# Two orders of work rewritten in an eight-layer kernel: the stores and loads beside the filters of the first mixer, and the pieces carried beside the scans of the last

## The chip, the cores and the metric

The kernel runs on one core of a Trainium2 chip, as one program. The metric is device microseconds of one execution on that core, lower being better. The time of a kernel is the median of several runs; for the kernel before there are three.

## What is computed

Eight layers follow one another on `x` of shape (8, 512, 256): eight sequences of 512 tokens with 256 features. Each layer `f` adds to the residual, and layernorm stands on both sides of it:

```python
x = x + _layernorm(f(_layernorm(x, axis=-1), *weights), axis=-1)
```

There are four pairs of a mixer and a feed-forward layer. Two mixers, and the feed-forward layer between the third mixer and the fourth, matter here. The first mixer has three causal filters of 3, 15 and 63 taps for each of its 256 features, a delta rule in chunks whose triangular matrix is inverted, and a softmax gate over five paths that mixes the results:

```python
local_s, local_m, local_l = _fir(v_direct, fir_s), _fir(v_direct, fir_m), _fir(v_direct, fir_l)
...
        T = solve_triangular(M, jnp.broadcast_to(eye, M.shape), lower=True)
...
o = probs[..., 0:1] * local_s + probs[..., 1:2] * local_m + probs[..., 2:3] * local_l \
    + probs[..., 3:4] * delta_out + probs[..., 4:5] * v_direct
```

The last mixer is a selective state space model with 512 channels (DI) and 16 states. For each sequence:

```python
xr = x @ W_in.T
xc, res = (xr[..., :DI], xr[..., DI:])
u = silu(causal_conv4(xc) + b_conv)
x_dbl = u @ W_xproj.T                       # dt (16), B (16), C (16)
delta = softplus(dt @ W_dt.T + b_dt)
dA = exp(delta * A);  dBu = delta * B * u   # for each state n
h = dA_t * h + dBu_t                        # over the tokens t, for each channel and state
y = sum over n of h * C  +  u * D
out = (y * silu(res)) @ W_out.T
```

(The last block is shortened from the reference.) The feed-forward layer ahead of it, called the guest below, is `h = silu(x @ wg.T) * (x @ wu.T)`, `out = h @ wd.T`, with integer weights that are scaled by 1/127. All arithmetic is float32.

## The kernel before

The kernel keeps `x` in SBUF and writes out the program layer by layer. PE, DVE, ACT, POOL and SP each run their own list of instructions in order, and wait on semaphores for one another. Transfers are issued from SP's list, and some from ACT's. A scheduler puts the traced instructions into those lists. Two means of the code fix parts of the order. `behind()` (L375) asks that what is traced under it comes, on SP, DVE, ACT and POOL, after the instruction of that engine that was traced last. `in_order()` (called at the end of `l3_attn`) makes the order in which the last mixer is traced the order of the lists of PE, DVE, ACT and POOL.

**The filter stage** is in `l0_attn`. Its loop runs over G = 32 groups `g`. `filters(g)` does 16 matmuls of 128x256 elements (L661) into two PSUM tiles, multiplies each by its gates on DVE (`pr`, L666), loads the band matrix of group g + 3 (`load_band`: SP issues 256 KB at L452 and 320 KB at L455), adds the parts on POOL (`s1` L672, `s2` L674) and stores `s2` by two DMAs that ACT issues (L676). The first two bands have buffers of their own; the others share three, by g modulo 3. Beside the filters the loop carries, under `behind()`, other parts of the mixer:

- `scaled_v` (ACT L645, store L648): one tile `vs` a step.
- `strengths(1)` (iterator `late`), `gates`, `query_scales`, `value_scales`: small work on row vectors.
- `inverse(g)` (L328), a generator that `next()` advances piece by piece. It inverts the triangular matrices of one half of the sequences. Its pieces are: loads (SP L331, 2 MB, and a small one); one and then another DVE instruction; 15 pieces that hold two pairs of DVE instructions each; a last DVE product that yields True; the upper triangle cleared on POOL (affine_select L361) and the diagonal copied (L364); a 2 MB store from SP (L366) together with the first of four transposed copies on ACT (`tt`, L369) and its 512 KB store from ACT; and the other three copies and stores, one a piece.
- The first half's inverse is done up to True before the stage. In the stage, `inv` is advanced in steps g = 1 (affine_select), 5 (2 MB store and first transposed store) and 6, 7, 8 (the other three); the call of step 9 ends it. In step 7 the second half's `inverse(1)` starts with its loads, and from step 11 on it advances by one piece a step, on DVE.
- In step 10 the loads for the next stage are issued: `load_tt` for sequences 0 and 1 (POOL memsets L413 and L414, two SP loads L417 each) and `load_blocks` (SP L426, L429, L432).

**The last mixer** is `l3_attn`. It runs the eight sequences one after another, each in 32 steps p: two halves h of the channels, times 16 states n. A step k of the whole chain does, in this order: `fetch(k + 4)` (SP loads the rows C and B, spread over the partitions); `scan(k, 0)`, for the first 128 channels, that is a decay dA on ACT (L2069, into PSUM pool `pA` with two buffers) and the scan on DVE (L2081); `spread(k + 2)`, the product dB; about half of the list `now`; `scan(k, 1)`; `weigh(k)`, the product with C on POOL (L2085, 2.4 us); the rest of `now`; the `pieces(b, p)` of the step; and `summed(k - 2)`, transposes on PE that add up y in PSUM (L2098). In `spread`, dB of n even, 7 or 15 is done on DVE (1.2 us), after ACT has copied B into PSUM (`pb`, L2062); for the other n it is done on POOL (2.4 us).

`pieces(b, p)` is a timetable. It names for each step the parts of other work that run beside the scans of sequence b: parts of b itself (`own`), of the next sequence a = b + 1 (`nxt`), of the one before, z = b - 1 (`last`: its gating, transposes and output projection), of the guest's sequence f = b + 2 (`ffn`), and of g = b + 3 (`later`). A part issues its matmuls at once and returns a list of functions for what follows them; these are the list `now` of the next step, and may return further lists for the step after. The order of the lists inside a step is the order in which `pieces` adds them: `last`, the burst of p = 22, `out`, `nxt`, `ffn`, `later`, `own`.

The parts that the change names or that work beside them are:

- `delta(b, c)`: one matmul (pd, L1967), then on ACT Abs, Relu and Exp (L1973, one step later), Identity and Ln (a step later), then three DVE instructions `third` (a step later). pd keeps its PSUM buffer until the third of these.
- `drive(b, h)`: du = delta * u on POOL.
- `turn_g(b, h)`: the transposes of the gated y on PE into two PSUM tiles pg, copied by ACT a step later.
- `project(b, m)`: eight matmuls (po, L2028), copied by ACT (L2031) a step later.
- `rest(b, h, m)`: the matmuls for `res`, copied a step later. `hidden(b, c, j)`: the guest's gate and up products (pf, L1883), copied by ACT (hid, L1889) a step later. `out_stats`, `norm_*` and `moments`: layernorm statistics on DVE, ACT and POOL (lnb, L1848); `scaled` (L1853): x times the scale on ACT.

All of these PSUM tiles (pd, pg, po, pf and the others tagged "mm") come from the pool `pmm` with three buffers. In step 22 `burst` does the decays of steps 23 and 24 ahead of time into SBUF tiles T[0] and T[1], and then all SiLUs of the next sequence and of the guest in one group on ACT. In step 23 the list `now` is held back by a step, and in step 24 its first function is put last.

Of the kernel before, what the change touches and what calls it, by code (L numbers as in the profile page):

```python
# [9 lines left out]
F32 = mybir.dt.float32  # L10
# [9 lines left out]
P = 128  # L20
NB = 8
# [253 lines left out]
def l0_attn(K):  # L275
    nc, tc = K.nc, K.tc
    w = K.W["l0_attn"]
    W = w[:, 0:2 * A_END].rearrange("p (k n) -> p k n", k=2)
    row = w[:, 2304:2332]
    H, J, G = 4, 8, 32  # L280
    HALF = NB // 2
    with ExitStack() as es:
# [152 lines left out]
        with ExitStack() as e1:  # L435
# [23 lines left out]
            with ExitStack() as ef:  # L459
                p1, p2, p3 = pool(ef, "a", 1), pool(ef, "b", 2), pool(ef, "d", 3)  # L460
# [102 lines left out]
                inv = iter(())  # L563
# [16 lines left out]
            with ExitStack() as ef:  # L580
# [13 lines left out]
                for g in range(2, 5):  # L594
                    load_band(g)

                gz = rw_all[:, 0:20, :].rearrange("p (h f) t -> p h f t", h=H)
# [44 lines left out]
                def scaled_v(b, n):  # L642
                    vs = p2.tile([P, H, 64], F32, tag="vs", name=f"vs{b}_{n}")
                    for h in range(H):
                        nc.scalar.mul(  # L645
                            vs[:, h, :], Vw[:, b, 2 * n + 1, 64 * h:64 * h + 64],
                            SSK[:, b, n, h:h + 1])
                    nc.scalar.dma_start(  # L648
                        out=v_d[b * P:(b + 1) * P, 256 * n:256 * n + 256],
                        in_=vs.rearrange("p h d -> p (h d)"))  # L650

                def filters(g):
# [19 lines left out]
                    nc.gpsimd.tensor_tensor(s1, pr[:, :, 0:2, :], pr[:, :, 2:4, :], ALU.add)  # L672
                    s2 = p2.tile([P, 4, 64], F32, tag="s2", name=f"s2_{g}")
                    nc.gpsimd.tensor_tensor(s2, s1[:, :, 0, :], s1[:, :, 1, :], ALU.add)  # L674
# [7 lines left out]
                for g in range(G):  # L682
                    filters(g)
                    with behind():
# [7 lines left out]
                        if g in (0, 4, 6):  # L692
                            next(late, None)
                        if g in (1, 5, 6, 7, 8, 9):
                            next(inv, None)
                        if g == 7:
                            inv2, inverted = inverse(1), False
                            next(inv2)
                        if g == 10:
                            assert next(inv, 0) == 0  # L700
                            for b in range(2):
                                load_tt(b)
                            load_blocks(0, TS0, T10)
# [1072 lines left out]
def l3_attn(K):  # L1776
# [10 lines left out]
    with ExitStack() as es:  # L1787
# [234 lines left out]
        def project(b, m):  # L2022
            R[b]["Y"] = flat(T[1])
            ps = pmm.tile([P, 2, D], F32, tag="mm", name=f"po{b}_{m}")
            for j in range(2):
                n = 2 * m + j
                for c in range(4):
                    nc.tensor.matmul(  # L2028
                        ps[:, j, :], lhsT=R[b]["g", c // 2][:, c % 2, n * P:(n + 1) * P],
                        rhs=W[:, c, M_OUT:M_OUT + D], start=(c == 0), stop=(c == 3))  # L2030
            return [lambda: nc.scalar.copy(R[b]["Y"][:, 2 * m:2 * m + 2, :], ps)]  # L2031

# [21 lines left out]
        def spread(k):  # L2054
            if k < len(order):
# [3 lines left out]
                on = nc.gpsimd  # L2059
                if n % 2 == 0 or n in (7, 15):  # L2060
                    pb = pB.tile([P, L], F32, tag="b", name=f"pb{b}_{h}_{n}")
                    nc.scalar.copy(pb, B)  # L2062
                    B, on = pb, nc.vector
# [63 lines left out]
        def pieces(b, p):  # L2127

            a, z, f, g = b + 1, b - 1, b + 2, b + 3
            own = {0: [(delta, b, 2)], 3: [(delta, b, 3), (open_sums, b, 0)],  # L2130
                   6: [(drive, b, 1), (rest, b, 1, 0)], 9: [(rest, b, 1, 1)],
                   19: [(open_sums, b, 1)], 20: [(turn_g, b, 0)]}
# [5 lines left out]
                   20: [(rest, a, 0, 0)], 21: [(rest, a, 0, 1)],  # L2138
                   23: [(rows_of, a)], 24: [(delta, a, 0)], 25: [(delta, a, 1)],
                   28: [(drive, a, 0)]}  # L2140
            ffn = {1: [(hidden, f, 0, 0)], 2: [(hidden, f, 1, 0)], 3: [(hidden, f, 2, 0)],
# [8 lines left out]
            if b == 0:  # L2150
                for p0, p1 in ((1, 6), (2, 7), (3, 8), (4, 9), (5, 10)):
                    ffn[p1] = ffn.pop(p0)
                ffn.update({0: [(norm_stats, f)], 1: [(norm_root, f)], 2: [(norm_apply, f)],
                            4: [(turn_x, f, "fT")]})
            last = {5: [(turn_g, z, 1)], 7: [(project, z, 0)], 8: [(project, z, 1)],
                    10: [(out_stats, z)], 12: [(out_add, z)]}
# [9 lines left out]
            if f < NB:  # L2166
                todo += ffn.get(p, [])
            if g < NB:
                todo += later.get(p, [])
# [500 lines left out]
```

## Time and profile before

| what | us |
|---|---|
| runs shown, median (lowest to highest of 3) | 4557.25 (4557.15 to 4561.31) |
| the profiled execution, its time | 4555.24 |
| the same execution, its span | 4553.5 |

The span reaches from the first instruction to the last of one profiled execution; the mean granted clock of TensorE in it is 0.93. Over the span PE is busy 3963.8 us (87%), DVE 2698.8 (59%), ACT 2016.2 (44%) and POOL 2118.9 (47%). By stretches of the span, in us of busy time:

| stretch | long | PE | DVE | ACT | POOL | DMA share |
|---|---|---|---|---|---|---|
| 0 to 239, front of the first mixer | 239.0 | 199.6 | 174.9 | 128.8 | 5.7 | 0.39 |
| 239 to 402, the filter stage | 163.0 | 122.2 | 122.7 | 44.1 | 83.2 | 0.72 |
| 402 to 690, the delta rule and after | 288.0 | 245.4 | 154.2 | 109.9 | 76.5 | 0.54 |
| 690 to 2657, layers between | 1967.0 | 1772.7 | 1030.3 | 803.2 | 830.6 | 0.18 |
| 2657 to 2793, opening of the last mixer | 136.4 | 103.2 | 28.7 | 54.4 | 16.3 | 0.12 |
| 2793 to 3891, its eight sequences | 1097.6 | 898.5 | 967.8 | 731.5 | 941.4 | 0.38 |
| 3891 to the end, last layer | 662.5 | 622.2 | 220.3 | 144.3 | 165.3 | 0.50 |

"DMA share" is the mean busy share of the core's 16 DMA engines. The eight sequences of the last mixer take 146.9, 137.4, 136.4, 136.2, 136.6, 136.2, 150.0 and 117.9 us.

How to read the views: an instruction is named by its engine and line (DVE L2081), its output and inputs, and its tile's shape. A timeline lists runs of like instructions with their start, their length, how many (x), and in square brackets the engine's idle time just before and what ended it. A list of waits adds up, for one kind of instruction, the idle time that one releaser ended: the total, how many times, and the longest. SPq is SP's own list, and an entry of it is the issue of a DMA. Matmuls are pipelined, so a busy PE is not always PE at its peak.

### The profile page before, as it was taken

What the parts mean: (1) busy time and instruction counts of PE and PEld (TensorE: products, weight loads), DVE (VectorE), ACT (ScalarE), POOL (GpSimd) and SP (SyncE); (2) the same over time, 40 slices, a digit from 0 to 9 for tenths busy, and PEclk for the clock granted to TensorE, in tenths of its full rate; (3) what the DMA queues carried; (4) which work ended last, traced back from release to release, by engine and by line L of the source; (5) the groups of instructions that cost most, each with busy time, mean ns of one, the idle gap of its engine ahead of it and who ended that gap; (6) DMA issues with size and microseconds to landing.
All of it is one profiled execution on the core that took longest, in us unless ns stands there. A gap on an engine that the chain in (4) does not pass through costs nothing. (4 is left out here: it accounts for less than half of the span.)

```text
span 4553.5 us, 63426 instructions
## 1 busy us (share of the span) xinstructions
PE 3963.8 (87%) x21672; PEld 2633.7 (58%) x21672; DVE 2698.8 (59%) x7145; ACT 2016.2 (44%) x4210; POOL 2118.9 (47%) x2081
## 2 busy tenths in 40 slices
PE   8868888999998599699999978998888876899997
PEld 3435765555655499544554534565655545678884
DVE  7767656456757611255566534888888899721115
ACT  5532433444344233334444444767676655311112
POOL 0045222444344244344555423889988879223321
PEclk9889999999999799889999989899999886899999
DMA  4377621000000299400000002343433334336653
GB/s 120 94 218 189 179 62 63 5 5 7 7 10 16 69 254 251 130 5 10 6 6 6 1 23 68 123 125 126 127 122 122 124 110 136 103 118 234 228 180 113
DMA packets 392818, 442.90 MB, mean 97 GB/s; under 512 B 147853, under 2 KB 275967, under 8 KB 391983
## 3 DMA queue, kind: packets, MB, share of 16 engines
q1 hardware_dynamic: 361087, 390.18, 28.4%
q0 software_dynamic: 16272, 31.87, 2.6%
q10 hardware_dynamic: 15136, 16.80, 1.1%
q8 instruction: 172, 2.82, 0.3%
q14 instruction: 151, 1.24, 0.1%
HBM read 372.49 MB, written 66.26 MB: 96 GB/s over the span
## 5 line engine op out<-in xcount | busy, mean ns | idle before, releaser
L2085 POOL TENSOR_TENSOR h<-h,C 128x1024 f32<-128x1024 f32 x256 | 613.3, 2408 | 135.3 <-DVE h L2081 87.8
L2081 DVE TENSOR_TENSOR_SCAN h<-dA,dB 128x512 f32<-128x512 f32 x480 | 568.4, 1209 | 90.2 <-ACT dA L2069 73.9
L1039 POOL TENSOR_SCALAR p<-p,rs 128x128 f32<-128x128 f32 (+3 forms) x256 | 275.8, 1085 | 417.3 <-DVE rs L1038 261.1
L2069 ACT ACTIVATE dA<-dl,A 128x512 f32<-128x512 f32 x480 | 330.3, 690 | 174.4 <-DVE h L2081 173.7
L1605 DVE CUSTOM_DVE_ANT_0 junk<-S,mask 128x256 f32<-128x256 f32 (+3 forms) x512 | 249.5, 487 | 195.0 <-PE S L1599 156.7
L2098 PE MATMUL y<-C,h 128*128 128x128 f32 x2048 | 298.4, 297 | 68.0 <-POOL h L2085 67.9
L2098 PEld LDWEIGHTS y<-C,h 128*128 128x128 f32 x2048 | 263.2, 155 | 155.3 <-POOL h L2085 98.6
L1633 ACT ACTIVATE PT<-T 128x128 f32<-128x128 f32 (+3 forms) x512 | 198.0, 435 | 278.5 <-PE T L1628 267.6
L1599 PE MATMUL S<-KZ,QT 64*128 64x512 f32 (+3 forms) x1024 | 260.9, 492 | 23.9 <-DVE mx L1605 23.6
L2297 PE MATMUL gb<-xbT,w_b 128*128 128x256 f32 (+1 forms) x1472 | 255.3, 332 | 1.0 <-ACT ts L2501 0.6
L2297 PEld LDWEIGHTS gb<-xbT,w_b 128*128 128x128 f32 x1472 | 230.4, 191 | 22.8 <-ACT ts L2501 0.8
L2303 DVE TENSOR_TENSOR hTb<-sb,gb 128x512 f32<-128x512 f32 x71 | 48.8, 687 | 325.4 <-PE gb L2297 325.4
L2064 POOL TENSOR_TENSOR dB<-du,B 128x1024 f32<-128x1024 f32 x96 | 234.0, 2437 | 0.1
L1883 PE MATMUL pf<-fT,w_l_ffn 128*128 128x512 f32 x384 | 208.3, 681 | 26.5 <-ACT fT L1877 10.4
L1628 PE MATMUL T<-QT,KZ 64*128 64x384 f32 (+3 forms) x1024 | 216.7, 464 | 2.9 <-ACT PT L1633 2.5
L2064 DVE TENSOR_TENSOR dB<-du,pb 128x1024 f32<-128x1024 f32 x160 | 191.2, 1195 | 23.0 <-ACT pb L2062 21.2
L182 POOL TENSOR_TENSOR X<-X,yn 128x256 f32<-128x256 f32 (+1 forms) x56 | 79.4, 1436 | 255.3 <-ACT yn L177 213.9
L1373 ACT ACTIVATE hT<-h,w_l_ffn 128x128 f32<-128x128 f32 x384 | 109.5, 368 | 197.9 <-PE h L1368 197.9
L1368 PE MATMUL h<-xgT,w 128*128 128x128 f32 x1536 | 185.0, 279 | 0.0
L1636 POOL TENSOR_SCALAR_AFFINE_SELECT PT<-PT 128x512 f32<-128x512 f32 x128 | 81.2, 634 | 219.8 <-ACT PT L1633 206.8
L1599 PEld LDWEIGHTS S<-KZ,QT 64*128 64x128 f32 x1024 | 117.2, 193 | 113.9 <-issue 58.4
L2534 POOL DMA_INDIRECT ys<-yb,place x71 | 69.8, 984 | 238.7 <-ACT yb L2533 224.5
(605 smaller groups left out, 9266.5 us busy)
## 6 DMA issues: line engine op xcount, KB each, us to landing
w_b<-l3f_w SPq DMA_DIRECT2D x138, 512.0 KB
C<-xdd SPq DMA_DIRECT2D x256, 256.0 KB
B<-xdd SPq DMA_DIRECT2D x256, 256.0 KB
w<-l1f_w SPq DMA_DIRECT2D x48, 1024.0 KB
w<-l1f_w SPq DMA_DIRECT2D x48, 256.0 KB
band<-l0fd SPq DMA_DIRECT2D x30, 320.0 KB
X<-x SPq DMA_DIRECT2D x16, 512.0 KB
c<-ys SPq DMA_DIRECT2D x16, 512.0 KB
```

Source lines behind the costliest of these rows:

```text
L1039: nc.gpsimd.tensor_scalar(p[:, 0:n], p[:, 0:n], rs, None, ALU.mult)
L1599: nc.tensor.matmul(ps[:, 0:n], lhsT=QT[half, qt * P:n], rhs=KZ[half, j % 2, 0:n], start=True, stop=True)
L1605: nc.vector.tensor_tensor_reduce(out=junk[:, 0:n], in0=ps[:, 0:n], in1=mask[:, L - n:L], scale=1.0, scalar=-3.0e38, op0=ALU.add, op1=ALU.m ...
L1628: nc.tensor.matmul(ps[:, 0:n], lhsT=KZ[half, j % 2, kt * P:(kt + 1) * P], rhs=QT[half, kt * P:L], start=True, stop=True)
L1633: nc.scalar.activation(PT[:, j, :], ps[:, 0:n], AF.Exp)
L1883: nc.tensor.matmul(ps, lhsT=gu[:, k, j * 768 + c * P:j * 768 + (c + 1) * P], rhs=R[b]["fT"][:, k, :], start=(k == 0), stop=(k == 1))
L2064: on.tensor_tensor(dBs[k], R[b]["du", h], B[:, None, :].to_broadcast([P, 2, L]), ALU.mult)
L2069: nc.scalar.activation(dA, R[b]["dl", h][:, c, :], AF.Exp, scale=A[:, 2 * h + c, n:n + 1])
L2081: nc.vector.tensor_tensor_scan(hs[k][:, c, :], dA, dBs[k][:, c, :], 0.0, ALU.mult, ALU.add)
L2085: nc.gpsimd.tensor_tensor(hs[k], hs[k], row_C.pop(k)[:, None, :].to_broadcast([P, 2, L]), ALU.mult)
L2098: nc.tensor.matmul(R[b]["y", h][q // 2][:, q % 2, c * P:(c + 1) * P], lhsT=t[:, c, q * P:(q + 1) * P], rhs=K.ident, is_transpose=True, sta ...
L2297: nc.tensor.matmul(ps[:, q, :], lhsT=ww[:, k, (c + q) * P:(c + q + 1) * P], rhs=xT[:, k, :], start=(k == 0), stop=(k == 1))
```

## The change

It edits two functions and touches no arithmetic: the same products are made, two of them on another engine.

In the filter stage:

1. The piece of `inv` that holds the affine_select is advanced once before the loop, behind the loads of bands 2 to 4.
2. The other pieces of `inv` are advanced in steps 3, 5, 7 and 9 (2 MB store with the first transposed store, then the other three), and the call of step 11 ends it; before, in 5, 6, 7, 8 and 9.
3. `load_tt` and `load_blocks` are issued in step 13 instead of 10. The condition `g > 10` for the second inverse stays.
4. `vs` and `s2` have four buffers each instead of two.

In the last mixer:

5. `turn_g(z, 1)` moves from step 5 to 4, `project(z, 0)` and `project(z, 1)` from 7 and 8 to 6 and 7. The copy of the projection gets one more list around it, so it runs two steps after its matmuls instead of one, in steps 8 and 9 as before. `rest(b, 1, 0)` moves from 6 to 8.
6. `delta(a, 0)`, `delta(a, 1)` and `drive(a, 0)` of the next sequence move from steps 24, 25 and 28 to 25, 26 and 29, into a list `row` that is added behind the guest's list instead of ahead of it.
7. In half h = 1 the products of n = 10 and n = 11 change places: n = 10 (step 26, spread in step 24) goes to POOL without a copy pb, n = 11 (step 27, spread in step 25) to DVE with one.

```diff
--- before.py
+++ after.py
@@ -593,6 +593,8 @@
                     clear(bands[2 + i])
                 for g in range(2, 5):
                     load_band(g)
+                with behind():
+                    next(inv)
 
                 gz = rw_all[:, 0:20, :].rearrange("p (h f) t -> p h f t", h=H)
 
@@ -640,7 +642,7 @@
                     nc.vector.tensor_tensor(sk, sk, rk, ALU.mult)
 
                 def scaled_v(b, n):
-                    vs = p2.tile([P, H, 64], F32, tag="vs", name=f"vs{b}_{n}")
+                    vs = p2.tile([P, H, 64], F32, tag="vs", name=f"vs{b}_{n}", bufs=4)
                     for h in range(H):
                         nc.scalar.mul(
                             vs[:, h, :], Vw[:, b, 2 * n + 1, 64 * h:64 * h + 64],
@@ -670,7 +672,7 @@
                         load_band(g + 3)
                     s1 = s1s
                     nc.gpsimd.tensor_tensor(s1, pr[:, :, 0:2, :], pr[:, :, 2:4, :], ALU.add)
-                    s2 = p2.tile([P, 4, 64], F32, tag="s2", name=f"s2_{g}")
+                    s2 = p2.tile([P, 4, 64], F32, tag="s2", name=f"s2_{g}", bufs=4)
                     nc.gpsimd.tensor_tensor(s2, s1[:, :, 0, :], s1[:, :, 1, :], ALU.add)
                     for r in range(2):
                         nc.scalar.dma_start(
@@ -691,12 +693,12 @@
                         scaled_v(g // NT, g % NT)
                         if g in (0, 4, 6):
                             next(late, None)
-                        if g in (1, 5, 6, 7, 8, 9):
+                        if g in (3, 5, 7, 9, 11):
                             next(inv, None)
                         if g == 7:
                             inv2, inverted = inverse(1), False
                             next(inv2)
-                        if g == 10:
+                        if g == 13:
                             assert next(inv, 0) == 0
                             for b in range(2):
                                 load_tt(b)
@@ -2028,7 +2030,7 @@
                     nc.tensor.matmul(
                         ps[:, j, :], lhsT=R[b]["g", c // 2][:, c % 2, n * P:(n + 1) * P],
                         rhs=W[:, c, M_OUT:M_OUT + D], start=(c == 0), stop=(c == 3))
-            return [lambda: nc.scalar.copy(R[b]["Y"][:, 2 * m:2 * m + 2, :], ps)]
+            return [lambda: [lambda: nc.scalar.copy(R[b]["Y"][:, 2 * m:2 * m + 2, :], ps)]]
 
         def out_stats(b):
             R[b]["on"], chain = moments([R[b]["Y"][:, n, :] for n in range(NT)], "on")
@@ -2057,7 +2059,7 @@
                 dBs[k] = s3.tile([P, 2, L], F32, tag="dB", name=f"dB{b}_{h}_{n}")
                 B = row_B.pop(k)
                 on = nc.gpsimd
-                if n % 2 == 0 or n in (7, 15):
+                if (n % 2 == 0 or n in (7, 15)) != (h == 1 and n in (10, 11)):
                     pb = pB.tile([P, L], F32, tag="b", name=f"pb{b}_{h}_{n}")
                     nc.scalar.copy(pb, B)
                     B, on = pb, nc.vector
@@ -2128,7 +2130,7 @@
 
             a, z, f, g = b + 1, b - 1, b + 2, b + 3
             own = {0: [(delta, b, 2)], 3: [(delta, b, 3), (open_sums, b, 0)],
-                   6: [(drive, b, 1), (rest, b, 1, 0)], 9: [(rest, b, 1, 1)],
+                   6: [(drive, b, 1)], 8: [(rest, b, 1, 0)], 9: [(rest, b, 1, 1)],
                    19: [(open_sums, b, 1)], 20: [(turn_g, b, 0)]}
             out = {0: [(out_stats, a)], 2: [(out_add, a)]}
             nxt = {6: [(norm_stats, a)], 7: [(norm_root, a)], 8: [(norm_apply, a)],
@@ -2136,8 +2138,8 @@
                    14: [(taps, a, 0)], 15: [(into, a, 2)], 16: [(taps, a, 1)],
                    17: [(into, a, 3)], 18: [(taps, a, 2)], 19: [(taps, a, 3)],
                    20: [(rest, a, 0, 0)], 21: [(rest, a, 0, 1)],
-                   23: [(rows_of, a)], 24: [(delta, a, 0)], 25: [(delta, a, 1)],
-                   28: [(drive, a, 0)]}
+                   23: [(rows_of, a)]}
+            row = {25: [(delta, a, 0)], 26: [(delta, a, 1)], 29: [(drive, a, 0)]}
             ffn = {1: [(hidden, f, 0, 0)], 2: [(hidden, f, 1, 0)], 3: [(hidden, f, 2, 0)],
                    4: [(hidden, f, 3, 0)], 5: [(hidden, f, 4, 0)], 11: [(hidden, f, 5, 0)],
                    22: [(hidden, f, 0, 1)], 23: [(hidden, f, 1, 1)],
@@ -2152,7 +2154,7 @@
                     ffn[p1] = ffn.pop(p0)
                 ffn.update({0: [(norm_stats, f)], 1: [(norm_root, f)], 2: [(norm_apply, f)],
                             4: [(turn_x, f, "fT")]})
-            last = {5: [(turn_g, z, 1)], 7: [(project, z, 0)], 8: [(project, z, 1)],
+            last = {4: [(turn_g, z, 1)], 6: [(project, z, 0)], 7: [(project, z, 1)],
                     10: [(out_stats, z)], 12: [(out_add, z)]}
             todo = []
             if z >= 0:
@@ -2165,6 +2167,8 @@
                 todo += nxt.get(p, [])
             if f < NB:
                 todo += ffn.get(p, [])
+            if a < NB:
+                todo += row.get(p, [])
             if g < NB:
                 todo += later.get(p, [])
             if b < NB:
```

## The prediction

> **What bounds the kernel now.** The change has two places, so I read the page's forty slices to find them, then timelines of each engine inside them. The filter stage of the first mixer runs from 239 to about 402 us, the last mixer from 2793.4 to about 3890 us. No single engine bounds either.
>
> *Filter stage.* One filter step g is 16 matmuls. The timeline of PE, with the idle time before each run of them in brackets:
>
> ```profile
> 284.02 3.98 PE L661 MATMUL pf<-band,Vw 128*64 128x256 f32 x16 [1.69 <-DVE rw_all L600]
> 290.28 3.98 PE L661 MATMUL pf<-band,Vw 128*64 128x256 f32 x16 [2.28 <-DMA band<-l0fd]
> 303.47 11.40 PE L661 MATMUL pf<-band,Vw 128*64 128x256 f32 x48 [9.21 <-DMA band<-l0fd]
> 326.79 44.93 PE L661 MATMUL pf<-band,Vw 128*64 128x256 f32 x192 [11.91 <-DMA band<-l0fd]
> 376.19 11.42 PE L661 MATMUL pf<-band,Vw 128*64 128x256 f32 x48 [4.46 <-DVE pr L666]
> ```
>
> Twelve undisturbed steps take 44.93 us, so a step is 3.75 us; before step 14 PE stands 2.28 + 9.21 + 11.91 = 23.4 us for bands. Why the bands are late shows in the timeline of the SP queue, and in its waits (us in total, times, longest):
>
> ```profile
> 286.78 0.44 SPq L331 DMA_DIRECT2D X<-l0s  x1
> 297.39 0.32 SPq L452 DMA_DIRECT2D band<-l0fd  x1
> 306.35 6.04 SPq L417 DMA_DIRECT2D X<-l0tt  x4
> 318.55 0.33 SPq L426 DMA_DIRECT2D T<-l0t  x1
> 320.98 0.34 SPq L452 DMA_DIRECT2D band<-l0fd  x1
> ...
> SPq L452 <- DMA l0f<-s: 16.3, 6, 6.8
> SPq L426 <- DMA l0v<-vs: 6.1, 1, 6.1
> ```
>
> The reader is to see two things. From 275 to 305 us the 16 DMA engines are busy 1.01, 0.86 and 1.01 of three 10 us windows: the inverse's 2 MB store (issued 272.21), its four 512 KB transposed stores, the 2 MB load for the second half, all on top of 576 KB of band a step. And the load_tt and load_blocks of step 10 hold SP from 303.7 to 320.98, so the band of step 14 is asked for 17 us late. From 335 to 385 us DVE is busy without a gap: there the second inverse is the bound.
>
> *Last mixer.* I count its steps by pairs of scans; sequence 3 starts at 3214.05 and takes 136.3 us. In it DVE is busy 119.1 and POOL 119.9 us, so neither alone sets the time. ACT's order of work does, at two spots (steps 5 to 9, and 24 to 25):
>
> ```profile
> 3236.56 0.59 ACT L1973 ACTIVATE t<-pd 128x512 f32<-128x512 f32 x1
> 3237.03 0.59 ACT L1889 COPY hid<-pf 128x512 f32<-128x512 f32 x1
> 3237.50 0.72 ACT L2069 ACTIVATE dA<-dl,A 128x512 f32<-128x512 f32 x1
> ...
> 3253.20 0.59 ACT L2031 COPY t<-po 128x512 f32<-128x512 f32 x1 [3.15 <-PE po L2028]
> 3254.75 0.60 ACT L1853 ACTIVATE t<-X,lnb,lnh 128x256 f32<-128x256 f32 x1 [0.96 <-POOL lnb L1848]
> 3255.25 0.67 ACT L2069 ACTIVATE dA<-dl,A 128x512 f32<-128x512 f32 x1
> ...
> 3314.82 0.59 ACT L2062 COPY pb<-B 128x512 f32<-128x512 f32 x1
> 3315.35 0.69 ACT L2069 ACTIVATE dA<-dl,A 128x512 f32<-128x512 f32 x1
> 3320.54 0.69 ACT L1973 ACTIVATE t<-pd,w_l_attn 128x512 f32<-128x512 f32 x1 [4.50 <-PE pd L1967]
> ```
>
> At 3253.20 ACT waits for the projection, and a moment later for POOL's lnb; DVE's scan of step 9 stands 3.85 us behind both. At 3314.82 the copy pb comes out behind the burst of SiLUs, so DVE stands 2.78 us; then ACT waits 4.50 us for delta's matmul, which waits on PE for DVE's xd, and DVE loses 1.72 + 0.61 + 1.19 us more.
>
> **The filter stage, part by part.**
> - *Affine select before the loop.* It ran 4.06 us at 255.04, with POOL then idle 4.70 us for pr. Now it stands ahead of the first two sums, which end near 259 us either way: 0.
> - *Store at step 3 (was 5), transposed stores at 3, 5, 7, 9 (were 5 to 8).* Two megabytes leave about 8 us earlier, into 255 to 265 us, where DMA was busy 0.40. ACT's four copies (2.0 us each) and DMA bytes are the same. Of the 11.5 us lost at 290.28 and 303.47 I give back 7.5; bounds 0 (the 2 MB load at step 7 remains) and 11.5.
> - *Four buffers for s2 and vs.* POOL waits 11.9 us in seven places for the store of s2, ACT 11.7 us in four for that of vs. These waits delay the stores on which SP's bands wait (16.3 us above). Counted with the line before and after, nothing of its own.
> - *load_tt, load_blocks at step 13 (were 10).* Seven DMAs still pass through SP ahead of a band (17 instead of 14), but the last transposed store is then four steps old instead of two. The hold of 17.3 us loses X's waits for it (2.7 + 2.2 + 0.9) and, with the pipe not starved, most of the 6.1 + 3.8 us before T. What is left, some 5 to 8 us, is close to the three steps in hand (11.25 us) less a landing (about 5 us). So 8.5 to 10 of the 11.9 us come back; bounds 0 and 11.9.
> - Then DVE: from the second inverse's first instruction (308.10) to its last (406.3) it is busy 78 us, and that work is unchanged; it starts earlier by what PE won. The clearing of PE's waits by 7.5 + 9.5 makes **-17 us**, bounds -23.4 and 0.
>
> **The last mixer, steps 4 to 10** (sequences 1 to 5 have a projection and a guest). turn_g moves from step 5 to 4, in front of the guest's hidden product. PSUM tag "mm" has three buffers; delta's pd keeps one from 3228.96 until DVE's third at 3243.8. turn_g takes the other two, so hidden's matmuls must wait for ACT's first copy of pg. That copy stands at step 5 behind t<-pd, now at 3236.56 less 0.62 (the Ln goes before the decay), the decay and pg: first pg copy near 3237.2, done 3237.8; hidden 1.98 us on PE, 3239.8; copy of hid to 3240.3; the decay of step 6 to 3241.0 instead of 3238.2. DVE was ready at 3238.47: **it stands 2.5 us** where it stood for nothing. One of third's instructions (0.7 us) goes behind the scan, so POOL's weigh of step 6 starts 1.9 us later; POOL has no gap from there to lnb, so lnb is 1.8 later. The projection now is done early (its 3.15 us wait goes), but lnb comes next anyway, and one more x scaled before the decay and rest's copy add 0.5 + 0.5. Replayed to the scan of step 10: +2.2 us a sequence. Bounds: -0.7 (no stall at step 6) and +2.7.
>
> **Steps 24 to 31** (sequences 0 to 5). The product for n = 10 goes from DVE with its pb to POOL, n = 11 the other way: the 2.78 us wait for pb goes. Delta a step later and behind the guest takes 1.72 + 0.61 + 1.19 us of DVE's waits, since PE does two hidden products from 3316 on. What is late next: (a) the second early scan now runs beside POOL. The rows:
>
> ```profile
> 3304.99 4.42 DVE L2081 TENSOR_TENSOR_SCAN h<-t,dB 128x512 f32<-128x512 f32 x2
> 3310.92 1.75 DVE L2081 TENSOR_TENSOR_SCAN h<-t,dB 128x512 f32<-128x512 f32 x1
> 3316.59 1.22 DVE L2081 TENSOR_TENSOR_SCAN h<-t,dB 128x512 f32<-128x512 f32 x1
> ```
>
> Alone it takes 1.22; beside POOL 1.75, or 3.3 (the second of the pair). I take 2.5, between the two: 3312.67 to 3315.2. (b) Abs, Relu, Exp of delta now come just ahead of decays at steps 26 and 27: 1.1 + 1.2 us. (c) drive moves from 28 to 29. It must wait for delta's last product, about 3341.5, and behind the weigh of step 29 on POOL, whose scan ends 1.3 us before; weigh's 2.35 and its own 2.37 us make du ready near 3345, and DVE, after one scan (1.12), has to wait 2.3 us for it at step 30, where it waited for nothing. Replayed to the next sequence's first scan: 3349.5 instead of 3350.3. **-0.8 us** a sequence; bounds -3 (drive in time) and +0.7 (scan 3.3 us).
> [...]
>
> Sequence 6 has delta and no guest, sequence 7 neither: 0, within 3 us; there DVE also carries the router of the last layer.
>
> **Sum.** -17 + 5 x 2.2 - 6 x 0.8 = -10.8 us. The profiled execution took 4555.24 us (span 4553.5 and 1.7 around it), so it would be 4544.4; the runs' median is 2.0 above that execution, so **4546**.
>
> **Rivals.**
> - *The mixer wins too.* If the wait for pg at step 5 stays off DVE (-0.7 instead of +2.2) and du is in time (-3), it gives -3.5 - 18: with the filters about 4520 to 4525. For it: everything between steps 24 and 30 starts 2 to 4 us earlier. Against: three PSUM buffers.
> - *The hold only moves.* SP stalls at step 13 as it did at 10, and the DMA engines stay full until then: filters -5, mixer +6: 4558.
> - *Slower.* Place: ACT at step 5 and POOL at step 29. Price: +2.7 x 5 and +0.7 to +2 x 6 in the mixer, some +23 with sequence 6, and the filters give back less than 9: about 4571. It decides from the point where the waits for pg and du cost more than 3.5 us a sequence together.
> - *Not what it says.* behind() only asks that work come after; an order in which the affine select or the stores stay late gives the mixer's +6 alone, 4563. I count it with the second.
>
> **Chances.** Forecast 0.45 (its own range 4535 to 4553), mixer wins 0.20, hold moves 0.20, slower 0.15. About 0.2% (9.1 us) is what a measurement of this kernel tells from no change, so faster means below 4548.1: 0.30 + 0.20 + 0.02 = 0.52; slower, above 4566.4: 0.13; between, 0.35. The range 4520 to 4564 leaves out the slower rival and little else.
>
> **What would show it.** In the profile after: PE's gaps before steps 11 and 14 under 5 us, and the stage's end (the last L661 matmul, 400.1) near 384; ACT at step 5 waiting for pf, DVE 2 to 3 us idle before the scan of step 6; no wait of ACT for po; no pb wait at step 24; a DVE wait for du at step 30; sequences 1 to 5 at 137 to 138 us. A sequence under 134 us, or a gap over 8 us at step 17 of the filters, would prove me wrong.

## The result, and the profile after

The kernel after takes **4584.33 us** (median of 6 runs, 4582.32 to 4589.85), the kernel before, run beside it, 4560.4 (6 runs, 4557.15 to 4563.51). The ratio is 1.0056 [1.0045, 1.0067]: slower by about 24 us, where 4546 was forecast. It lies outside the range.

| from one profiled execution of each, us | before | after | forecast change |
|---|---|---|---|
| its time / its span | 4555.24 / 4553.5 | 4583.58 / 4581.8 | |
| last filter matmul ends | 400.1 | 403.4 | -17 |
| first scan of the last mixer starts | 2793.4 | 2801.5 | -17 |
| eight sequences, first scan to end of last | 1095.9 | 1116.6 | +6 |
| sequence 6 alone | 150.0 | 157.0 | 0 within 3 |

The profiled execution of before lies 5 us under the median of its six runs, so the spans differ by more than the medians. That is also why the first two rows need care: with before's filters untouched, two later kernels (e2 and e8) ended the stage at 400.7 and 403.0 and began the scans at 2802.4 and 2798.9. From the end of the stage to the first scan, where all kernels have the same code, the seventeen profiled executions take between 2393.3 us (before) and 2404.1 us (e9). The 20.7 us of the mixer are firm: ten kernels fall into two groups, below.

**The filter stage.** PE's timeline of the kernel after (start, length, instruction, in brackets PE's idle time before it):

```profile
277.45 3.97 PE L663 MATMUL pf<-band,Vw 128*64 128x256 f32 x16 [2.16 <-DMA band<-l0fd]
281.96 7.71 PE L663 MATMUL pf<-band,Vw 128*64 128x256 f32 x32 [0.55 <-issue]
293.11 3.98 PE L663 MATMUL pf<-band,Vw 128*64 128x256 f32 x16 [3.44 <-DMA band<-l0fd]
304.17 22.57 PE L663 MATMUL pf<-band,Vw 128*64 128x256 f32 x96 [7.08 <-DMA band<-l0fd]
341.55 33.76 PE L663 MATMUL pf<-band,Vw 128*64 128x256 f32 x144 [14.81 <-DMA band<-l0fd]
```

The gaps ahead of step 14 are 2.16 + 0.55 + 3.44 + 7.08 = 13.2 us; before they were 13.2 too (1.69 + 2.28 + 9.21). The second gap is still there, larger (14.81 for 11.91) and moved to step 17. The SP queue of the same kernel, and its waits (us in total, times, longest):

```profile
316.02 1.20 SPq L455 DMA_DIRECT2D band<-l0fd  x1
317.32 10.51 SPq L417 DMA_DIRECT2D X<-l0tt  x4
...
336.52 0.34 SPq L452 DMA_DIRECT2D band<-l0fd  x1
```

```profile
SPq L452 <- DMA l0f<-s: 14.3, 5, 5.2
SPq L333 <- DMA X<-l0s: 8.7, 1, 8.7
SPq L417 <- DMA l0f<-s: 8.0, 3, 3.3
```

From 316.02 to the next band at 336.52 SP is held 20.5 us by the seven loads, where the forecast was 5 to 8. Three of the four issues of X wait for stores of s2, which belong to ACT.

**The mixer, steps 4 to 6** of sequence 3. First DVE of the kernel before, where the two scans around the start of step 6 follow each other without a wait:

```profile
3237.34 2.33 DVE L2081 TENSOR_TENSOR_SCAN h<-dA,dB 128x512 f32<-128x512 f32 x2
```

Then PE, DVE and ACT of the kernel after:

```profile
3246.37 1.04 PE L2019 MATMUL pg<-C,sr 128*128 128x128 f32 x8
3250.64 3.46 PE L1885 MATMUL pf<-fT,w_l_ffn 128*128 128x512 f32 x4 [3.24 <-ACT t L2022]
```

```profile
3255.35 1.22 DVE L2083 TENSOR_TENSOR_SCAN h<-dA,dB 128x512 f32<-128x512 f32 x1 [4.07 <-ACT dA L2071]
```

```profile
3254.14 0.59 ACT L1891 COPY hid<-pf 128x512 f32<-128x512 f32 x1 [3.06 <-PE pf L1885]
```

Each link of the forecast is there: pg holds the two PSUM buffers that pd leaves, hidden's matmuls wait for the first copy of pg, ACT waits for hidden, and the decay (it starts at 3254.62) stands behind its copy. But DVE stands 4.07 us, not 2.5, because the four matmuls take 3.46 us, in which the granted clock of TensorE is 0.55 on average, where they took 1.88 in the kernel before.

**Steps 24 to 30** of the same sequence, DVE:

```profile
3327.59 4.97 DVE L2083 TENSOR_TENSOR_SCAN h<-t,dB 128x512 f32<-128x512 f32 x2
...
3343.39 1.22 DVE L2083 TENSOR_TENSOR_SCAN h<-dA,dB 128x512 f32<-128x512 f32 x1 [0.53 <-ACT dA L2071]
3347.41 1.23 DVE L2083 TENSOR_TENSOR_SCAN h<-dA,dB 128x512 f32<-128x512 f32 x1 [1.06 <-ACT dA L2071]
3361.61 1.22 DVE L2066 TENSOR_TENSOR dB<-du,pb 128x1024 f32<-128x1024 f32 x1 [2.40 <-POOL du L1993]
```

The second scan of the pair takes 3.31 of the 4.97 us (forecast 2.5), the two waits for decays 0.53 and 1.06 (1.1 and 1.2), the wait for du 2.40 (2.3).

After minus before, by sequence, from the starts of the scans (us):

| steps | 0 | 1 | 2 | 3 | 4 | 5 | 6 | 7 | forecast for 1 to 5 |
|---|---|---|---|---|---|---|---|---|---|
| 4 to 10 | 0.85 | 0.87 | 2.10 | 3.94 | 3.02 | 3.50 | -2.28 | -1.54 | 2.2 each |
| 11 to 23 | -0.4 | 0 | 0 | 0 | 0 | 0 | 7.29 | 0.89 | 0 |
| 24 to 31 | -1.27 | 1.29 | 1.13 | -0.87 | 0.85 | -0.92 | 1.86 | 0.33 | -0.8 each |

### The profile page after: what moved, and what is told of

Same layout as the page of the kernel before. It is cut to its first block, busy times and chain, and to the rows that moved or that the text cites. A ratio compares the mean times of both kernels' runs of the same rounds, so it can differ in the third digit from the quotient of the medians.

```text
span 4581.8 us, 63436 instructions
## 1 busy us (share of the span) xinstructions
PE 3968.3 (87%) x21672; PEld 2636.3 (58%) x21672; DVE 2711.0 (59%) x7145; ACT 2017.3 (44%) x4210; POOL 2125.9 (46%) x2081
```

## The experiments

The questions: which edit costs how much; why the filters gave nothing back; why some sequences lose more than others; and why sequence 6 loses 7 us. "Stage" is the end of the last filter matmul, "mixer" the length of the eight sequences, both from one execution.

| kernel | median (runs) | before | ratio [95%] | stage | mixer |
|---|---|---|---|---|---|
| before | | | | 400.1 | 1095.9 |
| after | 4584.33 (6) | 4560.4 | 1.0056 [1.0045, 1.0067] | 403.4 | 1116.6 |
| e1_filters_only | 4570.6 (11) | 4561.17 | 1.0015 [1.0006, 1.0024] | 406.4 | 1096.8 |
| e2_mixer_only | 4583.5 (5) | 4561.17 | 1.0048 [1.0034, 1.0061] | 400.7 | 1117.3 |
| e3_turn_behind | 4572.6 (10) | 4561.17 | 1.0025 [1.0015, 1.0034] | 403.7 | 1101.1 |
| e4_loads_spread | 4576.68 (6) | 4561.17 | 1.0035 [1.0023, 1.0048] | 395.8 | 1117.2 |
| e5_combo | 4557.71 (11) | 4564.08 | 0.9987 [0.9978, 0.9996] | 397.2 | 1094.8 |
| e6_merged_stores | 4612.04 (4) | 4564.08 | 1.0106 [1.0091, 1.0121] | 425.6 | 1117.9 |
| e7_load_early | 4581.56 (5) | 4564.08 | 1.0037 [1.0024, 1.0051] | 400.3 | 1117.1 |
| e8_rows_only | 4560.79 (11) | 4564.08 | 0.9990 [0.9981, 0.9999] | 403.0 | 1096.8 |
| e9_split_stores | 4585.92 (4) | 4558.84 | 1.0059 [1.0044, 1.0074] | 399.6 | 1117.3 |
| e10_combo_early | 4564.51 (11) | 4558.84 | 1.0012 [1.0003, 1.0021] | 404.2 | 1097.4 |
| e11_loads_on_act | 4582.57 (4) | 4558.84 | 1.0054 [1.0038, 1.0069] | 400.5 | 1117.7 |
| e12_old_filters_spread | 4562.86 (11) | 4558.84 | 1.0009 [1.0000, 1.0018] | 404.1 | 1094.6 |
| e13_store_twice | 4595.35 (4) | 4558.77 | 1.0079 [1.0063, 1.0095] | 411.8 | 1116.8 |
| e14_seq6_last_old | 4563.03 (10) | 4558.77 | 1.0010 [1.0001, 1.0020] | 403.9 | 1096.2 |
| e15_warm | 4580.38 (5) | 4558.77 | 1.0046 [1.0032, 1.0061] | 401.9 | 1114.5 |

Where the mixer is the change's, it takes 1116.6 to 1117.9 us, whatever the filters; where it is before's, 1095.9 and 1096.8. With the change's filters and nothing else altered in them, the stage ends at 401.9 to 406.4 (after, e1, e3, e14, e15: mean 403.9); with before's, at 400.1 to 403.0 (before, e2, e8: mean 401.3).

### Which half costs: e1 and e2

e1 is before with edits 1 to 4, e2 before with edits 5 to 7.

> Only edits 1 to 4 (filter stage); the last mixer as before. Theory A, the two places add up: in the changed kernel the filter stage ends 3.3 us later (first L774 matmul 404.3 instead of 400.95) and the work up to 2740 us is 5.2 us late, so this kernel is 5 us slower than before (ratio 1.001), or 8 if the slow TensorE clock that the changed kernel shows at 2775 to 2787 us comes with it. Rival, the filter stage is innocent and all of the loss is the last mixer's: no difference from before.

> Only edits 5 to 7 (last mixer); the filter stage as before. Theory A: sequences 1 to 5 at 139 to 140 us instead of 136 to 137 (13 to 15 us in all), sequence 6 some 7 us longer, so 20 us slower than before (ratio 1.0045). Rival, sequence 6 only fell badly because everything before it was late: 13 us slower.

The mixer's edits alone give +0.48%, the filters' alone +0.15%, and after +0.56%. Sequence 6 is 6.9 us longer in e2 as well. It is so in e4 too (157.0 us), whose scans begin at 2791.5, ahead of the kernel before, so it is no effect of a later start. The filters win nothing by themselves; their cost is small, and the runs of e1 lie far apart (4560.05 to 4580.22), which no experiment here explained.

### The chain at step 5: e3

The guest's hidden product goes ahead of the transposes again, both in step 4.

```diff
-            last = {4: [(turn_g, z, 1)], 6: [(project, z, 0)], 7: [(project, z, 1)],
+            last = {6: [(project, z, 0)], 7: [(project, z, 1)],
...
+            if z >= 0 and p == 4:
+                todo.append((turn_g, z, 1))
```

> The whole change, but turn_g(z, 1) is issued at step 4 behind the guest's hidden product instead of ahead of it. Theory B: the loss at steps 5 and 6 is the hidden product waiting for ACT's copies of pg (three PSUM buffers) and then running at half the TensorE clock; with the order exchanged DVE's wait of 4.07 us ahead of the scan of step 6 is under 1, sequences 1 to 5 come down by 2.5 us each, the kernel to 4572. Rival, the loss comes from the projection and rest that were moved: DVE's wait moves to steps 8 to 10 and the kernel stays at 4584.

4572.6: 12 us less than after. DVE's wait in step 6 of sequence 3 falls from 4.07 to 1.21 us. Hidden no longer waits for pg, so PE stands no 3.24 us there. Steps 24 to 31 of sequences 0 to 5 now give -1.27, -0.41, -0.58, -0.87, -0.85 and -0.94, together -4.9 us: the forecast's -4.8. In after the gain fails in sequences 1, 2 and 4. There PE's eight matmuls for the guest in step 25 take 5.40 us instead of 3.70, and the granted clock is 0.50 for 3.41 us of them (lines under "The clock", at the end).

### A slow clock after the stall: e15

The stall at step 5 could have left the slow clock. To keep PE busy while it waits, the second tile's transposes are done five times over (same result).

```diff
-                for n in range(NT):
+                for n in range(NT * (5 if h and c else 1)):
+                    n = n % NT
```

> The whole change, but the transposes of the second tile of turn_g(z, 1) are done five times over (the same result; 16 more of 0.11 us, which end before ACT copies the tile). Theory B2: at step 5 TensorE stands 3.2 us for the copies of pg in sequences 3 to 5 and its clock is halved just then, so that the hidden product takes 3.5 us instead of 2.0; with TensorE idle for only 1.5 us the clock stays, as in sequences 1 and 2 (gap 1.6): step 5 falls from 6.9-7.5 to 6.1 us in sequences 3 to 5, some 4 us in all, 4580. Rival: the delay there has nothing to do with the clock: no change at step 5, 4584, or more for the added work.

4580.38. Step 5 takes 6.07 to 6.11 us in each of sequences 1 to 5, where after has 6.07, 6.06, 7.54, 6.94 and 7.41. PE and DVE of e15 in sequence 3:

```profile
3242.84 2.78 PE L2020 MATMUL pg<-C,sr 128*128 128x128 f32 x24
3245.50 1.98 PE L1885 MATMUL pf<-fT,w_l_ffn 128*128 128x512 f32 x4
```

```profile
3248.74 1.23 DVE L2084 TENSOR_TENSOR_SCAN h<-dA,dB 128x512 f32<-128x512 f32 x1 [2.63 <-ACT dA L2072]
```

Hidden takes 1.98 us again and DVE stands 2.63, the forecast's 2.5. The wait for pg costs 2.6 us; the other 1.4 of sequence 3 are the clock. Sequence 3 alone would not show it: its wait is 2.6 us in e2, e4, e6, e7 and e11 too. But each of the eight other kernels with this order has one to three of the five sequences at 3.3 to 4.1 us, and e15 has none.

The loss in steps 24 to 31 stays, though: e15 has +0.2 us there in all, as after has. So the stall at step 5 is not its cause; e8, below, has that loss without the stall.

### The loads on SP: e4 and e11

e4 spreads the seven loads over three steps; e11 issues them from ACT's list instead of SP's.

```diff
 # e4
-                            for b in range(2):
-                                load_tt(b)
+                            load_tt(0)
+                        if g == 15:
+                            load_tt(1)
+                        if g == 17:
                             load_blocks(0, TS0, T10)
 # e11
-                                load_tt(b)
-                            load_blocks(0, TS0, T10)
+                                load_tt(b, nc.scalar)
+                            load_blocks(0, TS0, T10, nc.scalar)
```

> The whole change, but the seven loads of step 13 are spread: load_tt of sequence 0 in step 13, of sequence 1 in step 15, load_blocks in step 17. [...]

> The whole change, but the seven loads of step 13 are issued from ACT's list instead of SP's, where the bands are issued. Theory C1: the hold of 20 us is SP's list, in which the bands stand behind the seven loads; from ACT's list they hold only the stores of s2 and vs, the gap of 14.8 us at step 17 falls under 5 and the stage ends 8 us earlier, 4576. [...]

e4: 4576.68, the stage 7.6 us earlier. So the hold is one of place: the same loads, with bands between them, cost less. e11 takes the gap away almost altogether, and wins only 2.9 us, which is less than the kernels with the change's filters scatter (401.9 to 406.4). PE's timeline of e11:

```profile
335.95 18.84 PE L663 MATMUL pf<-band,Vw 128*64 128x256 f32 x80 [0.63 <-DMA band<-l0fd]
...
367.27 3.98 PE L663 MATMUL pf<-band,Vw 128*64 128x256 f32 x16 [4.78 <-DVE pr L668]
```

The 14.81 us at step 17 are 0.63, and from 358 on PE waits for DVE instead: the gaps of steps 25 to 31 grow from 5.3 to 10.8 us. DVE, with the second inverse, is the next bound.

### The gaps ahead of step 14: e7, e9, e6 and e13

Three causes were open: the 2 MB load of the second half, the number of DMAs that SP and ACT wait on in turn, and the bytes. e7 issues the load at step 2; e9 stores s2 in four DMAs of half the rows instead of two; e6 in one; e13 stores the inverse's 2 MB a second time.

```diff
 # e7: inverse yields between its two loads for the second half
+                        if g == 2:
+                            inv2, inverted = inverse(1), False
+                            next(inv2)
                         if g == 7:
-                            inv2, inverted = inverse(1), False
                             next(inv2)
 # e9, the stores of s2
-                    for r in range(2):
+                    for q in range(4):
+                        r, m = q // 2, 32 * (q % 2)
 # e13, in the step that stores the inverse
+                        if g == 0:
+                            nc.sync.dma_start(out=t2_d, in_=flat)
```

> The whole change, but the second inverse's 2 MB load is issued at step 2 instead of step 7. [...] Rival, the load only takes the same DMA time earlier: equal gaps at steps 5 to 8, 4584.

> [...] Rival, the bytes alone bound the stage: 4584.

> The whole change, but the two stores of s2 of each filter step are one DMA of the same bytes. [...] Rival, bytes in flight bound the stage: nothing changes, 4584.

> The whole change, but the 2 MB store at step 3 is followed by a second one of the same 2 MB to a place that nobody reads. Theory E (the 16 DMA engines' bytes set the bands' lateness at steps 5 to 13): 2 MB at the 375 GB/s of 290 to 300 us are 5.6 us, which come on top of the 13.2 us of gaps there; the kernel is at 4588 to 4590. Rival: the engines have room (their share is 0.85 from 270 to 300 us) and the lateness is that of single waits: gaps of 13 to 14 us as before, 4584.

e7 moves the gaps and keeps their sum nearly: 11.9 us in steps 5 to 13 for 13.2. e9 doubles the stores' number and the gaps do not grow (over the stage 9.6 + 11.8 + 13.6 + 4.3 = 39.3 us in e9, 9.4 + 13.2 + 14.8 + 5.3 = 42.7 in after), so the number is not what they cost; its time is no better, since ACT now ends its part of the stage 3.1 us later (its last `vs` at 412.19 instead of 409.11). e13 adds 2 MB, and the gaps of steps 5 to 13 grow by 9.2 us, to 22.4. PE of e13:

```profile
288.15 11.43 PE L666 MATMUL pf<-band,Vw 128*64 128x256 f32 x48 [11.91 <-DMA band<-l0fd]
300.28 3.98 PE L666 MATMUL pf<-band,Vw 128*64 128x256 f32 x16 [0.70 <-DMA band<-l0fd]
314.04 22.57 PE L666 MATMUL pf<-band,Vw 128*64 128x256 f32 x96 [9.79 <-DMA band<-l0fd]
```

So more bytes make these gaps longer, and by more than the 5.6 us that the forecast worked out for the bytes alone. The SP queue shows how: e13 issues no band from 266.92 to 282.76, and 15.8 us of that are one wait for a store of s2, which landed late; the longest such wait of after is 5.2 us. The full DMA engines (in after their share is 1.02 from 290 to 300) and the waits of SP's list therefore act together, and no run here separates them. Moving a store moves no bytes out of the window. e6 did not answer its question: with one store in place of two the late stores landed 7 to 11 us after their issue instead of 2 to 4, and the stage ended at 425.6 instead of 403.4. Why one store of the same bytes took longer than two is not shown. It ended 0.5% above after, by the ratios, and does not bear on the number of DMAs.

### Sequence 6: e14, and rows alone: e8

e14 is e3 with the old places of turn_g, project and rest in sequence 6 only; e8 is before with edits 6 and 7 alone.

> The kernel with turn_g behind the hidden product (e3, 4572.6), in which sequence 6 alone has the old steps for turn_g, project and rest, but the new ones for delta and drive and the exchange. Theory: of the 7 us that sequence 6 lost, the pieces of the sequence before (project, rest) cost 4.5, because DVE used to do the last layer's statistics while it waited for ACT at step 9, and delta and drive 2.5 (e8): sequence 6 at 152.5 us, the kernel at 4568. Rival: delta and drive alone cost all of it in this company: 157 us, 4572.

> The kernel before with edits 6 and 7 alone (delta and drive a step later and behind the guest's products, n = 10 and 11 exchanged). Theory: -0.8 us for each of sequences 0 to 5, as forecast, which the changed kernel shows in sequences 0, 3 and 5 and hides elsewhere behind a slower TensorE clock left by the stall at step 5; sequence 6 0 to +2: 4557 to 4560. Rival: the steps 24 to 31 lose about 1 us in some sequences by themselves (du late, clock): 4565.

e14 takes 152.3 us for sequence 6: 4.6 of the 6.9 come from edit 5, 2.3 from edits 6 and 7; e8 has +2.5 there. The place is visible on DVE at step 15, first one line of before, then two of after:

```profile
3700.72 1.47 DVE L95 TENSOR_TENSOR lnw<-lnw,lny 128x4 f32<-128x4 f32 x1
...
3724.11 2.23 DVE L95 TENSOR_TENSOR lnw<-lnw,lny 128x4 f32<-128x4 f32 x1
3726.66 1.97 DVE L96 SCALAR_TENSOR_TENSOR lny<-lnw,lny 128x4 f32<-128x4 f32 x1
```

Instructions on four numbers a partition take about 2 us each, where most of their like take 0.15. These are layernorm statistics of the last layer, which the kernel does not pin to a step, so a new order of the mixer's pieces can put them between other scans. Before has such long ones too. In step 9 these statistics, begun while DVE waits for ACT, keep DVE busy 10.7 us in before and 5.6 in after, in step 15 3.1 and 7.8. Step 9 itself gets shorter (12.73 to 9.01 us), and what it no longer holds comes later. Step 15 takes 9.84 us (before 5.16, e14 5.16), step 17 10.18 (9.38, 9.36), step 19 4.08 (2.24, 2.24).

e8 is at 4560.79, just above its forecast, but its steps 24 to 31 refute the theory of its expectation. It has no stall at step 5, and sequences 0 to 5 change by -1.27, -0.40, +1.12, +0.84, -0.86 and +0.79: together +0.2, as in after. What decides is where the slow clock falls. In every kernel with edits 6 and 7 and in each of sequences 1 to 5, the loss (+0.8 to +1.3 us) stands where the guest's eight matmuls take 5.4 us, and the gain (-0.40 to -0.95) where they take 3.7.

### The version that combines them: e5, e10, e12

e5 is e3 with e4, and all old places in sequence 6. e10 is e5 with the load at step 2 and the loads at steps 13, 16 and 19. e12 is e5's mixer with before's filters, loads spread at steps 10, 12 and 14.

> The whole change with three places mended: turn_g behind the hidden product, the seven loads spread over steps 13, 15 and 17, and in sequence 6 the old timetable (old steps for turn_g, project, rest, delta and drive, old exchange of products). Theory D: the loss of 7 us in sequence 6 comes from what the change does in that sequence, where DVE also carries the last layer's statistics; with the old timetable it is back at 150 us. With the filter stage 4 us shorter, sequences 0 to 5 about as before (0 to -1 each) the kernel is at 4552 to 4558, at or under before. Rival: the last layer's statistics are placed by the scheduler wherever the rest of the program leaves them, so sequence 6 stays at 157 us whatever its timetable, and the kernel is at 4563.

> The mended kernel of before this (e5: hidden ahead of turn_g, loads spread, sequence 6 as it was) with the second inverse's 2 MB load at step 2 instead of 7 and the spread loads at steps 13, 16 and 19. Theory: the load at step 2 gave 3 us by itself, a wider spread another 2 to 4 of the 9 us of gaps that are left behind step 13: 4552. Rival: DVE with the second inverse is the bound from step 17 on, so that nothing more is won: 4558.

> The last mixer of e5 with the filter stage of before, in which only the loads of step 10 are spread over steps 10, 12 and 14. Theory: edits 1, 2 and 4 of the filter stage are worth nothing (before steps 8 to 12 TensorE stands 13.2 us for bands with and without them); the spread alone brings the stage's end to 397 and the kernel to the 4557 of e5. Rival: the earlier stores help once the hold is gone, and this kernel is 5 us slower than e5, 4563.

**e5 comes out ahead of both**: 4557.71, 0.9987 [0.9978, 0.9996]. That is below the 0.2% which the prediction named, but its interval excludes no change. So does that of e8 (0.9990 [0.9981, 0.9999]), whose profiled execution is no shorter than that of before at either place; the lead of e5 over before is small and, with that, not firm. Its gaps in steps 25 to 31 are 0.8 us, and sequence 6 loses 1.1. e10 is slower than e5: its gaps in those steps are 8.5 us, a wait for DVE, so the earlier load and the wider spread together win nothing. e12 ends the stage at 404.1 for e5's 397.2, and is slower (1.0009 against 0.9987; the intervals do not meet, though the runs of before beside them are on another chip). But e12 differs from e5 in two ways, the stores' places and buffers and the steps of the loads (10, 12 and 14 instead of 13, 15 and 17); which of them helps once the loads are spread is open.

## Why the prediction was wrong, point by point

- **Filters, "of the 11.5 us I give back 7.5"**: failed, nothing came. The gaps ahead of step 14 are 13.2 us as before. The view had shown the DMA engines full from 275 to 305 (a share of 0.96 over these 30 us); I treated the store as if it could leave earlier into the free stretch of 255 to 265, but it left at 265.10, and from 265 to 275 the engines are then 0.95 busy. The 2 MB load and the bands still pass behind it. e13 shows that bytes count, e7 that the load's place alone hardly changes the sum.
- **Filters, "what is left, some 5 to 8 us"**: failed, and this was the largest term. The hold is 20.5 us, the gap 14.81. I had taken X's waits of 2.7 + 2.2 + 0.9 us to be for the transposed stores alone. That was a misreading: in before, only 2.2 of them were, 2.7 were for X's own loads and 0.9 for a store of s2. After, they are for stores of s2, which ACT issues in every step, so there is always a recent one to wait for (X: 8.0 us in three issues). No view shows why an issue of SP waits for a store of ACT; that SP's list is the place is shown (e11, e4).
- **"Second inverse starts earlier by what PE won"**: empty, since PE won nothing before it: its first instruction is at 308.79, before at 308.10. What e11 wins behind it, DVE takes back. Sum of the filters: about +2.6 us by the stage's means, +0.15% (some 7 us) by the runs of e1, for -17.
- **Affine select and four buffers at 0**: not tested alone; POOL's waits for the stores of s2 are gone and no time with them.
- **Mixer, steps 4 to 10**: mechanism right, size +13.4 in sequences 1 to 5 for +11. The mis-sized term is hidden's 1.98 us: in sequences 3 to 5, where the clock is halved, it is 2.86 to 3.46. With PE kept busy, DVE's wait is 2.60 to 2.63 us for 2.5, and the five sequences lose 9.8 us. Sequence 1 loses little (0.87) because before has a slow clock there (0.50 from 2955.76 to 2962.59): its own step 5 takes 4.95 us, where its sequences 2 to 5 take 3.4.
- **Mixer, steps 24 to 31**: +0.2 in after for -4.8. The step that failed is that the sum has no term for TensorE's clock: where the guest's products of step 25 run at half clock (sequences 1, 2 and 4), PE's late end goes on to delta, and the steps lose 0.85 to 1.29 us instead of gaining. e3 has -4.9 because the slow clock misses these products in all its sequences. That is the forecast's mechanism at full clock, and luck in the number: e10, with the same order there, has +1.30 in sequence 1. The second early scan took 3.31 us where I took 2.5, and the sum of the undisturbed sequences still agrees with the forecast, since the decays' waits were smaller than I took (0.53 and 1.06 us for 1.1 and 1.2).
- **Sequence 6, "0, within 3 us"**: failed by 7. "There DVE also carries the router of the last layer" was seen, and no price put on moving it.
- **The slower rival** named the right places in the mixer, ACT at step 5, and its +23 is near the +20.7. That nearness is partly luck: steps 24 to 31, for which it had +0.7 to +2 a sequence, cost +0.2 in all, and sequence 6 cost 7. It still credited the filters with up to 9 us, so its 4571 is 13 too low.

Open: how much the filters really cost, given the scatter of single executions, and why e1's runs lie 20 us apart.

## What to carry to other kernels

Here a store moved 7 us ahead won nothing, since the window behind it stayed as full; and a burst of DMAs in a shared issue list cost less when the urgent loads went between its members: count what each issue would wait for at its new place, other engines' stores included. Before putting a product ahead of another, count the PSUM buffers, and price the wait with the next matmuls at half clock as well (here 2.86 to 3.46 us for 1.98). Where a planner places unpinned work between the steps, moving pieces moves that work too, and the steps that carry it are where the loss may lie.

## What the runs showed of the hardware

**The clock.** In the traces of before and after TensorE's granted clock comes in stretches of 3.413 us or whole multiples of it, each at 1.0 or 0.5 (145 of 146 stretches in before and 153 of 154 in after; the last one of each has another length). Stalls of 2.0 to 3.2 us were followed by matmuls that start 0.85 us apart instead of 0.43, but not every time. Here are px, the product x_dbl of the next sequence, and the guest's eight matmuls of step 25 in the kernel after, in sequence 1 and in sequence 3:

```profile
3044.13 3.63 PE L1950 MATMUL px<-u,w_l_attn 128*48 128x512 f32 x8 [2.38 <-ACT u L1944]
3052.59 5.40 PE L1885 MATMUL pf<-fT,w_l_ffn 128*128 128x512 f32 x8 [2.04 <-DVE xd L1958]
...
3324.76 5.33 PE L1950 MATMUL px<-u,w_l_attn 128*48 128x512 f32 x8 [2.38 <-ACT u L1944]
3333.20 3.70 PE L1885 MATMUL pf<-fT,w_l_ffn 128*128 128x512 f32 x8 [0.31 <-DVE xd L1958]
```

In sequence 1 the eight matmuls took 1.7 us more, with the clock at 0.50 from 3053.03 to 3056.44; in sequence 3 it was px, with the clock at 0.50 from 3326.10 to 3329.51, and there DVE was busy until 3332.5 with the scans ahead of its copy xd, so that the delay cost nothing. Why a stall had this price at one time and not at another was not shown. The waits of DVE ahead of step 6 in sequences 1 to 5 of after, which are alike in their work, are 2.60, 2.59, 4.07, 3.48 and 3.94 us. A sequence of e3 takes 136.5 us, 40 times 3.413, and shows the same picture each time, while those of after take 138.8 to 140.4, 40.7 to 41.1 times, and the picture changes. What a stall costs may thus depend on where it falls between the starts of the stretches: that is an estimate from these lengths, and no run tests it.

**Small work beside POOL.** In sequence 6 most VectorE instructions of 128x4 elements took 0.12 to 0.4 us, some of them beside POOL. But 11 of 39 in before and 13 of 39 in after took 0.9 to 2.3 us, and each of these ended within 0.03 us of the end of a POOL instruction of 2.34 to 2.37 us.
